# Attention with ternary weights and a gated feed-forward on one core: two-bank places for the ramp's maxima, a new order of the first key chunks, and block work put at other steps

## The chip, the core and the metric

The kernel runs on one core of one Trainium2 chip. The metric is the device time of one execution in microseconds, median of three runs. The core has five engines that work side by side, each through its own queue in order: TensorE (PE; its weight loads are listed as PEld), VectorE (DVE), ScalarE (ACT), GpSimd (POOL) and SyncE (SP), whose queue here issues nearly all DMAs. TensorE writes its results to PSUM, eight banks of 128 partitions x 512 f32.

## The reference

For 4096 tokens of width 256, the kernel computes one attention layer and one feed-forward layer, each with a residual and a layer norm behind it. All inputs are f32.

```python
def quant4(x):                       # per token, 4 bits
    ma = max(max(abs(x), -1), 1e-6)
    return clip(round(x / ma * 7), -8, 7) * ma / 7
def ternary_weight(w):               # -1, 0, 1 times the row's mean magnitude
    thresh = 0.05 * mean(abs(w))
    return where(abs(w) < thresh, 0, sign(w)) * mean(abs(w), axis=1, keepdims=True)

proj = quant4(x) @ ternary_weight(Wqkv).T + b          # one projection for q, k and v
q = proj.reshape(N, 16, 16).transpose(1, 0, 2)         # head h: columns of every token
k = v = proj.reshape(16, N, 16)                        # head h: 256 tokens, cut in 16 parts
q, k = rotary(q), rotary(k)
att = (q @ U) @ (k @ U).T / sqrt(16)                   # 16 heads of 4096 x 4096
y = softmax(att) @ v
x = layernorm(x + quant4(y) @ ternary_weight(Wo).T)
h = silu((x @ w1.T) * s1) * ((x @ w2.T) * s2)          # 256 -> 1024
h = gelu((h @ h1.T) * hs1); h = gelu((h @ h2.T) * hs2)
x = layernorm(x + (h @ w3.T) * s3)
```

## The kernel before

The tokens are cut in eight blocks of 512 (`QB`, `NQB`). The heads go in pairs: a pair's two heads lie in partitions 0 to 63 and 64 to 127 of the keys (`kT`, 128 x 4096) and of a block of queries (`qT`, 128 x 512), so that products of the two use the two halves of the PE array. A unit is one pair and one block of queries; there are 64 units of 32 steps, a step for each 128 keys. Pair 0 comes first with all blocks, so units 0 to 7 are pair 0.

Scores are computed twice. `largest` (L623) takes the maxima: in each step one 128-query tile against 512 keys for both heads, two products into two PSUM banks (L632) and a `tensor_reduce` for each (L640); 32 such steps give the unit's row maxima. These are split in two parts (`largest_parts`, ScalarE and GpSimd, L652 and L653), turned on VectorE (L659), written to DRAM (`m_dram`, L664) and read back as rows (`m_rows`, L667). `weights` (L671) runs `LAG` = 40 steps behind: it subtracts the maxima and adds the scores in PSUM (L678, a two-bank place of pool `ps_sc`, of which there are two) and ScalarE takes the exponential of both heads at once (L686). `values` (L689) comes 4 steps later and adds up the products with v, in four strips (L700). Later `finish`, `turn`, `gather`, `add_strips` and `divide` bring the unit's result in order and to `y_dram`. Hence steps 0 to 39 have only the maxima; this stretch is the ramp.

The order of the work is written by hand: `at(step, f)` puts a function on the list of a step, and the loop at L952 calls a step's list in the order of its making, then `largest` and `weights`. A step's number fixes only each engine's own order; an engine runs ahead until an operand or a buffer holds it.

Queries and keys are not all there at the start. Block b is needed from unit b on, and is prepared in the unit before, from `first = 32 * (b - 1)`: the block's rows of x are loaded (`x_bufs`, two in turn), their maxima taken (`biggest`, `measure`), quantized on GpSimd (`integers`, L148 to L152), transposed (`transposed`, L158, L160), and projected (`even_odd`, L459, ScalarE L467, GpSimd L468 and L469). L468 needs the token scales, which `tables` sends through DRAM (`start_scales`: turned on VectorE, L442, written, L445, read back, L447) together with the block's table of angles (`load_tables`). GpSimd rotates them (`queries`, L484 to L492; `rotate_keys`, L510 to L513); `store_queries` (L497) writes the queries to `q_dram`, and `load_queries` (L583) reads them as the `qT` of a unit, four DMAs. `regroup_keys` moves the rotated keys, `times_g` multiplies them with U's Gram matrix (L529, ScalarE L531, VectorE L532), and `store_keys` (L570) writes them for the other pairs, eight DMAs of a block. `natural` (L170, L603) and `rest` (L606, L607, GpSimd) make the block's v. The matrices of block 0 are prepared ahead of step 0, by VectorE and ScalarE; `place_queries` and `place_keys` put its queries and keys in place by products with selecting matrices, 512 keys at a time (L558, L565), g = 0 to 7.

Three pools of PSUM are used: `ps_sc` (two places of two banks), `ps_av` (one bank) and `ps_1` (three banks), from which `largest` and all block work (`bank1`) take their banks. Pools with one buffer (`kprep`, `rot`, `quantp`) make a block's first writer wait for the last reader of the block before.

The weights of the output layer are made ternary ahead of step 0: `magnitudes` (ScalarE L101, four products with ones, L104) and `signs` (VectorE, L113 to L120). They are first used in `front_steps`, at the attention's end. After the units comes the feed-forward (L964 on).

Of the kernel before, what the change touches and what calls it, by code (L numbers as in the profile page):

```python
# [18 lines left out]
P = 128  # L19
# [18 lines left out]
def attn_ffn_kernel(  # L38
# [54 lines left out]
    alpha_o = const.tile([P, D], F32, name="alpha_o")  # L93
    bias_bc = const.tile([P, D], F32, name="bias_bc")
# [204 lines left out]
    with ExitStack() as actx:  # L299
# [40 lines left out]
        def set_up():  # L340

            nc.sync.dma_start(out=x_bufs[0], in_=x_t[:, ts(0, BT), :])
            tw = [ppool.tile([P, 2, D], F32, name=f"tw{i}", tag="pr") for i in range(2)]
            wabs = ppool.tile([P, 2, 2, D], F32, name="tabs", tag="pr")
            neg = ppool.tile([P, 2, 2, D], F32, name="tneg", tag="pr")
            nc.sync.dma_start(out=tw[0], in_=wqkvT.rearrange("(k p) o -> p k o", p=P))
# [14 lines left out]
            ps = magnitudes(tw[0], wabs[:, 0], bank1)  # L361
# [5 lines left out]
            nc.sync.dma_start(out=tw[1], in_=woT.rearrange("(k p) o -> p k o", p=P))  # L367
# [3 lines left out]
            for e in range(2):  # L371
                for k in range(2):
                    nc.tensor.matmul(
                        ps[:, D + e : D + e + 1],
                        lhsT=wabs[:, 0, k, e::2],
# [15 lines left out]
            signs(tw[0], neg[:, 0], ps, sgn_qkv, alpha_qkv)  # L391
            nc.vector.tensor_scalar(alpha2, ps[:, D : D + 2], 1.0 / D, None, ALU.mult)
            nc.vector.tensor_tensor(gmat, psg[:, :P], mask, ALU.mult)

            def output_weights():
                ps = magnitudes(tw[1], wabs[:, 1], bank1)
                return lambda: signs(tw[1], neg[:, 1], ps, sgn_o, alpha_o)

            return held, output_weights
# [148 lines left out]
        def place_keys(held, kT, g, banks={}):  # L548

            if g % 2 == 0:  # L550
                banks[0] = ps_sc.tile([P, 2, QB], F32, name="sc")
            ps = banks[0][:, g % 2]
# [70 lines left out]
        def largest(s):  # L623

            u, i = divmod(s, NKT)
            qt, ck = divmod(i, NKT // BT)
            if i == 0:
                mxs[u] = stat.tile([P, BT, 2, NKT // BT], F32, name="mx")
            ps = [ps_1.tile([P, 512], F32, name="ps1") for j in range(2)]
# [9 lines left out]
            for j in range(2):  # L639
                nc.vector.tensor_reduce(  # L640
                    mxs[u][:, qt, j, ck : ck + 1], ps[j], AX.X, ALU.max
                )
# [174 lines left out]
        with tc.manual_schedule():  # L817
# [6 lines left out]
            first_held, output_weights = set_up()  # L824
            even_odd(0, first_held, 0)
            even_odd(0, first_held, 1)
            output_signs = output_weights()
# [5 lines left out]
            times_g(0, first_held, 0)  # L833
            place_queries(first_held, qTs[0])
            place_keys(first_held, kTs[0], 0)
            output_signs()
            times_g(0, first_held, 1)
            for g in range(1, 8):
                at(g - 1, lambda g=g: place_keys(first_held, kTs[0], g))
# [4 lines left out]
            for b in range(1, NQB):  # L844
# [13 lines left out]
                else:  # L858
                    biggest(None)
                    for f in measure:  # L860
                        f()
# [311 lines left out]
```

## Time and profile before

| | |
|---|---|
| three runs | 3588.69 to 3589.31 us, median 3589.16 |
| the profiled execution | 3586.87 us, its span 3585.0 |
| mean granted clock of TensorE | 0.993 |
| PE busy | 3544.8 us (99%) |
| DVE busy | 3044.8 us (85%), of it L640 2550.0 |
| ACT busy | 2337.1 us (65%), of it L686 1991.6 |
| POOL busy | 432.2 us (12%) |
| DMA moved | 141.74 MB |
| first issues of `m_dram` (one for a unit, its step 35) | 82.08, 133.53, 184.34, 236.37, 289.39, 339.99, 390.29, 434.55, 478.07 us |

Times are counted from the span's start. A row of the timeline has the start, the time, the engine, the line, the operation, output and inputs, the shapes and, in brackets, how long the engine stood idle ahead of it and what ended this. Rows that follow each other closely are merged (x4); their time is then that of the whole row. A row of the waits has the sum, how often, and the longest. In the forty slices a digit is a tenth, and 9 stands for 90% or more. A busy PE is not PE at its peak, since matmuls are pipelined and their ends are modelled.

### The profile page before, as it was taken

Reading aid. Unit: us, or ns where it says so; the run is one execution under the profiler, and the core shown is the slowest. Engines: PE = TensorE matmul, PEld = TensorE weight load, DVE = VectorE, ACT = ScalarE, POOL = GpSimd, SP = SyncE. Lnnn points to the kernel's source line nnn. Section 1 sums busy time; section 2 is a strip of 40 time slices with the busy share of each in tenths; the row PEclk is TensorE's granted clock in tenths of the full one; section 3 lists DMA queues with packets and bytes.
Section 4 is the critical chain, followed back from the end, with each engine's and each line's share of the span. In section 5 each row is a group of like instructions: output and inputs, shape, how many; then the busy total and the mean of one; then the engine's idle time right before and its main releaser. Section 6 shows DMA issues by size and latency. Waiting matters only on the chain.

```text
span 3585.0 us, 61100 instructions
## 1 busy us (share of the span) xinstructions
PE 3544.8 (99%) x23824; PEld 1996.1 (56%) x23831; DVE 3044.8 (85%) x5612; ACT 2337.1 (65%) x2710; POOL 432.2 (12%) x525
## 2 busy tenths in 40 slices
PE   7999999999999999999999999999999999999998
PEld 4444455555555555555555555545555458888887
DVE  8888999999999999999999999999999945555554
ACT  2777777777777777777777777777777753333332
POOL 5766300000000000000000000000000010000000
PEclk7999999999999999999999999999999999999999
DMA  3343212111211121112111111211121130000000
GB/s 92 91 112 100 58 27 50 27 27 27 50 27 29 30 50 27 27 27 51 28 27 43 34 27 27 44 27 23 47 68 33 24 91 1 29 25 18 18 7 13
DMA packets 267634, 141.74 MB, mean 40 GB/s; under 512 B 184520, under 2 KB 243656, under 8 KB 266440
## 3 DMA queue, kind: packets, MB, share of 16 engines
q1 hardware_dynamic: 263512, 126.22, 14.3%
q0 software_dynamic: 3824, 11.54, 1.1%
q8 instruction: 189, 3.10, 0.4%
q14 instruction: 109, 0.89, 0.1%
HBM read 91.44 MB, written 42.07 MB: 37 GB/s over the span
## 4 chain that ended last, share of the span: by engine, by line
PE 93%; POOL 2%; DVE 2%; DMA 2%; ACT 0%; issue 0%; SPq 0%; POOLq 0%; ACTq 0%
PE av L700 27%; PE sc L678 25%; PE ps L632 21%; PE ps_mm L997 18%; DVE mx L640 1%; DMA qT<-q_dram 1%; DMA scale<-ma_dram 0%; PE ps L529 0%; DMA ma_dram<-ma_turned 0%; POOL eo L469 0%; POOL qk L492 0%; POOL eo L468 0%; DMA q_dram<-qk 0%; POOL rot L484 0%; POOL rot L485 0%
## 5 line engine op out<-in xcount | busy, mean ns | idle before, releaser
L640 DVE TENSOR_REDUCE mx<-ps 128x1 f32<-128x512 f32 x4096 | 2550.0, 683 | 147.4 <-PE ps L632 93.1
L686 ACT ACTIVATE pr<-sc 128x1024 f32<-128x1024 f32 x2048 | 1991.6, 1021 | 739.4 <-PE sc L678 737.2
L632 PEld LDWEIGHTS ps<-kT,qT 64*128 64x128 f32 x4096 | 567.3, 184 | 985.2 <-DVE mx L640 852.1
L700 PE MATMUL av<-pr,v_all 128*32 128x512 f32 x8192 | 1091.6, 605 | 0.7
L632 PE MATMUL ps<-kT,qT 64*128 64x512 f32 x4096 | 1064.5, 474 | 10.0 <-DMA qT<-q_dram 4.0
L678 PE MATMUL sc<-m_rows,minus 64*128 64x512 f32 x4096 | 821.6, 394 | 0.4 <-DMA m_rows<-m_dram 0.4
L678 PE MATMUL sc<-qT,kT 64*128 64x512 f32 x4096 | 816.3, 392 | 0.0
L678 PEld LDWEIGHTS sc<-m_rows,minus 64*128 64x128 f32 x4096 | 392.6, 185 | 88.0 <-ACT pr L686 36.1
L678 PEld LDWEIGHTS sc<-qT,kT 64*128 64x128 f32 x4096 | 392.9, 184 | 86.7
L700 PEld LDWEIGHTS av<-pr,v_all 128*32 128x32 f32 x8192 | 161.3, 108 | 256.6 <-issue 254.7
L1027 ACT ACTIVATE gate<-ps_mm,sc_hs 128x512 f32<-128x512 f32 x128 | 88.1, 689 | 288.7 <-PE ps_mm L997 248.6
L281 DVE CAST h<-gate 128x512 fp32r<-128x512 f32 x128 | 54.3, 425 | 223.6 <-ACT gate L1027 223.4
L653 POOL TENSOR_TENSOR m_parts<-m,m_parts 128x8 fp32r<-128x8 f32 x64 | 13.0, 203 | 1798.7 <-ACT m_parts L652 1763.5
L283 DVE TENSOR_TENSOR h<-gate,h 128x512 fp32r<-128x512 f32 x192 | 132.3, 689 | 5.1
L997 PE MATMUL ps_mm<-h,h1a 128*128 128x512 f32 x512 | 128.8, 394 | 0.0
L1019 DVE SCALAR_TENSOR_TENSOR gate<-ps_mm,sc_s,gate 128x512 f32<-128x512 f32 x64 | 48.0, 750 | 94.3 <-ACT gate L1017 74.3
L997 PE MATMUL ps_mm<-h,h2a 128*128 128x512 f32 x512 | 127.2, 390 | 0.0
L997 PE MATMUL ps_mm<-h,h1b 128*128 128x512 f32 x512 | 126.5, 389 | 0.0
L997 PE MATMUL ps_mm<-h,h2b 128*128 128x512 f32 x512 | 126.5, 389 | 0.0
L732 DVE STREAM_TRANSPOSE yt<-ya 128x64 f32<-128x64 f32 x504 | 116.8, 232 | 0.0
L997 PEld LDWEIGHTS ps_mm<-h,h1b 128*128 128x128 f32 x512 | 96.1, 188 | 20.1
L997 PEld LDWEIGHTS ps_mm<-h,h2b 128*128 128x128 f32 x512 | 96.1, 188 | 19.9
(178 smaller groups left out, 1636.8 us busy)
## 6 DMA issues: line engine op xcount, KB each, us to landing
y_raw<-yt SPq DMA_DIRECT2D x256, 64.0 KB
qT<-q_dram SPq DMA_DIRECT2D x252, 64.0 KB
y<-y_raw SPq DMA_DIRECT2D x63, 256.0 KB
kT<-k_dram SPq DMA_DIRECT2D x28, 512.0 KB
xs<-in_x SPq DMA_DIRECT2D x16, 512.0 KB
q_dram<-qk SPq DMA_DIRECT2D x32, 256.0 KB
k_dram<-qk SPq DMA_DIRECT2D x56, 128.0 KB
cs_q<-in_csq SPq DMA_DIRECT2D x8, 512.0 KB
```

Source lines behind the costliest of these rows:

```text
L281: eng(dst[:, k, 0, :], g)
L283: nc.vector.tensor_tensor(dst[:, k, 1, :], g, dst[:, k, 0, :].bitcast(F32), ALU.subtract)
L632: nc.tensor.matmul(ps[j], lhsT=qTs[u][rows, ts(qt, P)], rhs=kTs[u // NQB][rows, ts(ck, 512)], start=True, stop=True,)
L640: nc.vector.tensor_reduce(mxs[u][:, qt, j, ck : ck + 1], ps[j], AX.X, ALU.max)
L653: nc.gpsimd.tensor_tensor(parts[:, :, 1, :], m, parts[:, :, 0, :].bitcast(F32), ALU.subtract)
L678: nc.tensor.matmul(ps[:, j, :], lhsT=minus[rows, :] if first else kTs[u // NQB][rows, ts(kt, P)], rhs=m_rows[u % 2][rows, :] if first else ...
L686: nc.scalar.activation(pr, ps, AF.Exp)
L700: nc.tensor.matmul(avs[u][strip : strip + 32, :], lhsT=v_all[:, 2 * (2 * pair + j) + a, c * (DK + 1) : c * (DK + 1) + 32], rhs=probs[s + k ...
L732: nc.vector.transpose(yts[u][:, ts(i, 64)], yas[u][:, ts(i, 64)])
L997: nc.tensor.matmul(ps, lhsT=sb[:, ks, ts(o, P)] if split else wo[:, k, :], rhs=src[:, k, i, :], start=(k == 0 and i == 0), stop=(k == n - ...
L1019: nc.vector.scalar_tensor_tensor(g, pb, scales["s2"][:, o : o + 1], gate, ALU.mult, ALU.mult)
L1027: nc.scalar.activation(g, ps, AF.Gelu, scale=scales[sc][:, o : o + 1])
```

## The change

- In the ramp (steps below 40) `largest` takes a two-bank place of `ps_sc` instead of two banks of `ps_1`, and one `tensor_reduce` takes the maxima of both heads from it. Later steps are as before.
- In unit 0 the maxima go by key chunk (four query tiles of a chunk, then the next chunk) instead of by query tile. `place_keys` uses `bank1`, and chunk g is placed at step 2g - 2 instead of g - 1.
- The output weights are loaded at step 3, into a tile of the pool `quantp`; their sums are taken at step 20 (ScalarE, TensorE, ScalarE), and their signs at step 288 on GpSimd.
- The second block's rows are measured and quantized ahead of `place_queries`; the first block's second `times_g` goes to step 5, its `rest` to step 34, its `natural` to steps 0 and 2, its `store_queries` to step 3.
- A block's steps come from a table `t`, with rows for block 1, block 2 and the others: tables, transposed, two even_odd, queries, store_queries, rest, natural, rotate_keys, regroup_keys. `integers` of block 2 goes from -1 to +2. `load_queries` of units 3 to 7 goes from 25 to 22.

```diff
@@ set_up, and a new output_weights
-            tw = [ppool.tile([P, 2, D], F32, name=f"tw{i}", tag="pr") for i in range(2)]
...
-            nc.sync.dma_start(out=tw[1], in_=woT.rearrange("(k p) o -> p k o", p=P))
...
-            def output_weights():
-                ps = magnitudes(tw[1], wabs[:, 1], bank1)
-                return lambda: signs(tw[1], neg[:, 1], ps, sgn_o, alpha_o)
...
+            def load():
+                held["w"] = quantp.tile([P, 2, 2, D], F32, name="two", tag="yb")
+                nc.sync.dma_start(
+                    out=held["w"][:, 0], in_=woT.rearrange("(k p) o -> p k o", p=P)
+                )
+            def sums():
+                ps = magnitudes(held["w"][:, 0], held["w"][:, 1], bank1)
+                nc.scalar.activation(
+                    alpha_o, ps[:, :D], AF.Copy, scale=1.0 / D, accum_out=total_o
+                )
+            def steps():
+                w, a = held["w"][:, 0], held["w"][:, 1]
+                th = stat.tile([P, 1], F32, name="tth")
+                nc.gpsimd.tensor_scalar(th, total_o, 1.0 / D, 0.05, ALU.mult, ALU.mult)
+                nth = stat.tile([P, 1], F32, name="tnth")
+                nc.gpsimd.tensor_scalar(nth, th, -1.0, None, ALU.mult)
+                nc.gpsimd.tensor_scalar(a, w, nth, None, ALU.is_le)
+                nc.gpsimd.tensor_scalar(w, w, th, None, ALU.is_ge)
+                nc.gpsimd.tensor_tensor(sgn_o, w, a, ALU.subtract)
@@ place_keys
-            if g % 2 == 0:
-                banks[0] = ps_sc.tile([P, 2, QB], F32, name="sc")
-            ps = banks[0][:, g % 2]
+            ps = bank1([P, QB], F32)
@@ largest
-            qt, ck = divmod(i, NKT // BT)
+            qt, ck = divmod(i, NKT // BT) if u else divmod(i, BT)[::-1]
...
-            ps = [ps_1.tile([P, 512], F32, name="ps1") for j in range(2)]
+            both = ps_sc.tile([P, 2, QB], F32, name="sc") if s < LAG else None
+            ps = [
+                ps_1.tile([P, 512], F32, name="ps1") if both is None else both[:, j]
+                for j in range(2)
+            ]
...
+            if both is not None:
+                nc.vector.tensor_reduce(mxs[u][:, qt, :, ck], both, AX.X, ALU.max)
+            else:
+                for j in range(2):
+                    nc.vector.tensor_reduce(
+                        mxs[u][:, qt, j, ck : ck + 1], ps[j], AX.X, ALU.max
+                    )
@@ the order
-            output_signs = output_weights()
...
+            h, biggest, measure, integers, transposed = quantize_steps(
+                x_bufs[1], bank1, nc.gpsimd, ma_parts[1][:, :BT]
+            )
+            biggest(None)
+            for f in measure:
+                f()
+            integers()
+            second = h, transposed
             place_queries(first_held, qTs[0])
             place_keys(first_held, kTs[0], 0)
-            output_signs()
-            times_g(0, first_held, 1)
             for g in range(1, 8):
-                at(g - 1, lambda g=g: place_keys(first_held, kTs[0], g))
-            at(2, lambda: store_queries(0, first_held))
+                at(2 * g - 2, lambda g=g: place_keys(first_held, kTs[0], g))
             for i in range(2):
-                at(4 + i, lambda i=i: natural(0, first_held, 2 * i))
-            at(6, lambda: [f() for f in first_held["rest"]])
+                at(2 * i, lambda i=i: natural(0, first_held, 2 * i))
+            at(3, lambda: store_queries(0, first_held))
+            at(5, lambda: times_g(0, first_held, 1))
+            at(34, lambda: [f() for f in first_held["rest"]])
+            load, sums, steps = output_weights()
+            at(3, load)
+            at(20, sums)
+            at(NKT * (NQB + 1), steps)
...
-                at(first - 1 if b > 1 else 0, integers)
-                at(first + 5, tables)
-                at(first + 7, transposed)
+                    at(first + 2 if b == 2 else first - 1, integers)
...
+                t = {
+                    1: (0, 3, 5, 6, 7, 21, 36, 13, 16, 29),
+                    2: (9, 11, 13, 15, 16, 24, 21, 17, 20, 30),
+                }.get(b, (-2, 5, 7, 9, 10, 21, 15, 11, 14, 28))
+                at(first + t[0], tables)
+                at(first + t[1], transposed)
                 for o in range(2):
-                    at(first + 9 + 2 * o, lambda b=b, h=h, o=o: even_odd(b, h, o))
-                at(first + 12, lambda b=b, h=h: queries(b, h))
-                at(first + 23, lambda b=b, h=h: store_queries(b, h))
+                    at(first + t[2 + o], lambda b=b, h=h, o=o: even_odd(b, h, o))
+                at(first + t[4], lambda b=b, h=h: queries(b, h))
+                at(first + t[5], lambda b=b, h=h: store_queries(b, h))
                 for i in range(2):
-                    at(first + 13 + 2 * i, lambda b=b, h=h, i=i: natural(b, h, 2 * i))
-                at(first + 16, lambda b=b, h=h: rotate_keys(b, h, nc.gpsimd))
-                at(first + 17, lambda h=h: [f() for f in h["rest"]])
-                at(first + 29, lambda h=h: regroup_keys(h))
+                    at(first + t[7] + 2 * i, lambda b=b, h=h, i=i: natural(b, h, 2 * i))
+                at(first + t[8], lambda b=b, h=h: rotate_keys(b, h, nc.gpsimd))
+                at(first + t[6], lambda h=h: [f() for f in h["rest"]])
+                at(first + t[9], lambda h=h: regroup_keys(h))
...
-                    at(NKT * (u - 1) + (25 if u < NQB else 14), lambda u=u: load_queries(u))
+                    at(NKT * (u - 1) + (25 if u < 3 else 22 if u < NQB else 14), lambda u=u: load_queries(u))
```

## The prediction

> **What bounds the kernel now.** I read the forty slices of the page first, then windows cut at the places where the work changes, then the timelines of the engines over the first 140 us, and the waits from 90 to 440 us. A step is one pass of the loop at L952; 32 steps are a unit; step 0 begins at 29.15 us.
>
> ```profile
> PE   7999999999999999999999999999999999999998
> DVE  8888999999999999999999999999999945555554
> POOL 5766300000000000000000000000000010000000
> PEclk7999999999999999999999999999999999999999
> ```
>
> TensorE is full from slice 2 on and VectorE nearly so until the attention ends. Only the first five slices (448 us) have GpSimd work, and only there does the diff move anything.
>
> ```profile
> 29.15:41.30 12.15, 11.01 (x72) 8.04 (x72) 9.56 (x17) 5.41 (x12) 8.21 (x9) 1.00 0.02 3
> 41.30:75.90 34.60, 32.04 (x74) 14.80 (x73) 33.50 (x60) 4.48 (x9) 31.68 (x29) 0.64 0.32 91
> 75.90:89.30 13.40, 11.98 (x27) 4.59 (x26) 9.98 (x19) 1.37 (x3) 4.67 (x5) 0.50 0.14 44
> 184.30:236.40 52.10, 50.20 (x345) 24.20 (x344) 44.04 (x86) 36.65 (x45) 35.40 (x32) 1.00 0.55 134
> 434.60:478.10 43.50, 43.50 (x322) 21.60 (x322) 41.47 (x75) 32.80 (x38) 4.47 (x5) 1.00 0.14 33
> ```
>
> Columns: window, length, busy PE, PEld, DVE, ACT, POOL, granted clock, DMA share, GB/s. The first three rows are the ramp (steps 0 to 39), where only maxima are taken: from 41.30 to 75.90 VectorE works 33.50 of 34.60 us, so it sets the pace there, and TensorE is granted half its clock from about 51 us. The fourth row is a unit that also prepares a block of queries and keys (52.10); the fifth is a plain one (43.50, TensorE never idle).
>
> ```profile
> 20.75 1.22 DVE L485 TENSOR_TENSOR rot<-eo,cs_q 128x1024 f32<-128x1024 f32 x1
> 53.84 2.48 DVE L640 TENSOR_REDUCE mx<-ps 128x1 f32<-128x512 f32 x4 [0.63 <-PE ps L632]
> 22.19 2.04 PE L529 MATMUL ps<-keys,gmat 128*128 128x512 f32 x2 [3.56 <-DMA keys<-rk]
> 27.17 1.02 PE L529 MATMUL ps<-keys,gmat 128*128 128x512 f32 x2
> 82.11 2.07 PE L529 MATMUL ps<-keys,gmat 128*128 128x512 f32 x2
> ```
>
> Four maxima in a row take 2.48 us: 0.69 for the last and 0.597 from one to the next. The same product takes 1.02 us at full clock and 2.07 in the ramp's last third; by its 2.04 at 22.19 the start runs at half clock too.
>
> ```profile
> 148.28 1.27 POOL L468 TENSOR_TENSOR eo<-eo,scale 128x512 f32<-128x512 f32 x1 [15.03 <-DMA scale<-ma_dram]
> 182.73 1.04 POOL L152 TENSOR_SCALAR qint<-qtmp 128x1024 bf16<-128x1024 f32 x1
> 183.85 0.21 POOL L653 TENSOR_TENSOR m_parts<-m,m_parts 128x8 fp32r<-128x8 f32 x1
> ```
>
> ```profile
> 136.23 5.12 SPq L570 DMA_DIRECT2D k_dram<-qk  x8
> 141.46 0.53 SPq L445 DMA_DIRECT2D ma_dram<-ma_turned  x1
> 144.97 0.36 SPq L447 DMA_DIRECT2D scale<-ma_dram  x1
> ```
>
> ```profile
> PE ps L632 <- DMA qT<-q_dram: 4.0, 3, 1.7
> DVE m_turned L659 <- POOL m_parts L653: 2.9, 4, 1.2
> ```
>
> In a block, GpSimd waits 15.03 us for the scales, whose request stood behind eight key stores in SP's queue (5.12 us), then works 35.6 us without a pause, and the unit's maxima (`m_parts`) come last in its queue. Their two late products, queries (`qT`) and maxima, stop TensorE and VectorE (last two lines).
>
> **The change, part by part.** Start. VectorE loses the output weights' signs (five operations, 25.50 to 27.94) and does the second block's maxima there instead (1.21, 0.16, 0.18 us from 25.6). TensorE loses one L104 group (2.08) that lay beside VectorE work. With `times_g` gone from 27.17 and the two `place_keys` in banks of their own, step 0's products are done near 29.6, and its maxima start then instead of at 30.98: 1.3 us won.
>
> Steps 0 to 15. From 27.3 TensorE's queue holds seven `place_keys` (1.17 each: 8.2), sixteen pairs of L632 (0.47: 7.5), four `natural` (0.6: 2.4), the transposes (0.7), `times_g` (1.0), two `even_odd` (0.6: 1.2): 21.0 us, plus some 1.7 for the wait for GpSimd's `qint` at step 3 and for places: to 50.0, and the maxima end near 51.4. VectorE alone would need 29.6 + 16 x 1.14 + 0.7 = 48.6, so TensorE sets the pace here. Before, step 15 ended at 55.13: 3.7 won. The second block's `queries`, now at step 7, reuse the buffer that `place_keys` read until step 12; GpSimd comes to its first write there at 37.7 + 5.7 + 7.3 = 50.7 (from `even_odd` at step 5, by the rows from 148.28 on), after the last of them at 46, so it doesn't wait.
>
> The merged maximum, 128x2 from 128x1024, is not in the trace. From above: two of the old (1.195 from step to step). From below: L485's 128x1024, whose start is 1.14 after the like operation at 19.61. I take 1.14, the row of the same size; nothing excludes 1.20, since at half clock a place's round (1.22 for the maximum, 0.8 to 1.0 to refill it) comes to 1.0 to 1.1 for each of two places.
>
> [...]
>
> Steps 16 to 31: 16 x 1.14 = 18.2, plus 1.6 for the next block's maxima (four of 0.41 and two small), plus the output weights' sums: four L104 at half clock, 2.08 us in TensorE's queue. A pair of L632 there takes 0.8 (0.79 at 84.12); filling, sums and refilling take 0.85 + 2.08 + 0.85 against two maxima's 2.28: 1.5 us of stall. ScalarE's two operations (0.61, and 0.4 to 0.7 by L603 and L467 with 0.19 for the accumulator) have an idle engine. So step 31 ends near 72.7 instead of 75.69.
>
> The granted clock is 0.50 from 52 to 88 us with TensorE shown busy 3.3 to 4.0 us in every 4, so I take half clock. [...]
>
> Steps 32 to 39: 8 x 1.14, twice a `times_g` for which VectorE waits (2.07 + 0.59 ScalarE + 0.69 own, less what is filled ahead: 2.0 each), 0.5 of small ones: 13.7, to 86.5 instead of 91.28: 4.8 ahead.
>
> What takes over: block 2's chain on GpSimd. Its tables now stand at step 41, behind the key stores (81.8 to 86.9): `ma_turned` near 87.7, scales 7.5 later as before (89.99 to 97.45): 95.2. `even_odd` at step 45 comes at 94.6, 95.7 with ScalarE. GpSimd is free then: the first block's `rest` (5.5), `integers` (5.3) and the second's `rest` (5.5) follow `m_parts` at about 75 and end at 91.5. Then 35.6 us as before: `m_parts` at 131.3 instead of 133.05, while VectorE would come to `m_turned` at 86.5 + 40.8 (91.28 to 132.09 before) + 0.7 (the transposes, now behind step 40) = 128.0. So of 4.8 us 1.75 remain, and VectorE waits some 3 us for `m_parts`, with the maxima of the next steps queued behind, and TensorE behind those.
>
> Blocks 3 to 7. Scales are asked for at step -2, before the key stores, and GpSimd starts with step 7's `even_odd`, 14 us into the unit (12.7 us for seven steps of unit 2, 1.4 for product and ScalarE) instead of 21.7 (148.28 less 126.6). Queries then arrive 14 + 29 = 43 us into a unit of 50 (29 from GpSimd's start, 200.34, to `qT`, 229.3), and its chain, with `rest` (5.5) now before the end, leaves `m_parts` free. Both waits go. From `m_dram` issue to issue (133.53, 184.34, 236.37, 289.39, 339.99, 390.29, 434.55) the units last 50.81, 52.03, 53.02, 50.60, 50.30, 44.26. Without its 0.8 of `qT` wait the fifth is 49.5; the four before it have four L129 maxima more, which widen a step by 0.15 each: 50.1. Won: 0.7 + 1.9 + 2.9 + 0.5 + 0.8 = 6.8. The last holds only `times_g` and stays. TensorE's extra work is the same, only sooner; SP's wait for the write of `ma_dram` (3.5 us) ends before step 3 needs `m_dram`.
>
> The output signs on GpSimd: three of about 1.57 (L469) and two tiny ones, in a unit where it is busy 4.5 of 43.5 us and nobody waits; if they fell before an `m_parts`, 5 us once. The load of the weights is one issue of 0.5 on SP with nothing due behind it. Nothing else moves.
>
> Sum: 1.75 + 6.8 = 8.6. The profiled execution took 3586.87 (span 3585.0), so 3578.3; the median of the three runs is 3589.16, 2.3 above it, so 3580.6. A difference of 0.2% (7.2 us) is about what a measurement of this kernel can tell from none.
>
> **The rivals.** More: block 2's chain isn't last, because the sums don't stall and GpSimd starts three to five microseconds sooner; then the ramp's 4.8 to 6.3 pass through: 3574 to 3577. For it: three of my terms there are rounded up. Against: the scales' path of 7.5 us is all queue and transfer. 0.16.
>
> Less: the waits in blocks 3 to 7 are replaced rather than removed (scales early, but ScalarE, full of exponentials, hands over `even_odd` late, or SP stands at `load_queries`, now three steps sooner, with the regrouped keys behind it). Half of 6.8 is lost, and the ramp's 1.75 may go too: 3584 to 3588. For it: units two and six had few such waits and are still over 49.5. 0.17.
>
> Slower: TensorE doesn't get its full clock at 27 us. It rose just after the products of 22.19 to 27.33, and the change takes one product out behind them. At half clock the 21.0 us of steps 0 to 15 become 35 (`natural` 1.01 against 0.61) to 42 (L529), 14 to 21 us more, all ahead of block 2's chain: 3595 to 3601. It decides against the change if half clock lasts past about 40 us. Against it: `place_keys` follow without a pause. 0.09.
>
> **How the numbers follow.** The forecast (3577.5 to 3583) has 0.58, three quarters of it below 3582, which is 0.2% under the median. With the first rival that makes faster 0.60; the rest of the forecast and "less" make same 0.31; slower has 0.09. The range leaves out the slow case and the edge of the best: 3574 to 3588.
>
> **What would show it.** Right: 40 maxima 128x2 from 128x1024, 1.14 apart; L104's second group in the ramp at 2.08; `m_dram`'s second issue at 131 to 132.5 with VectorE waiting some 3 us for `m_parts` before it; no wait for `qT` or `m_parts` in later units, which last 49.5 to 50.3; scales issued before the key stores. Wrong: clock below 1.00 between 30 and 45 us; maxima 1.2 apart or more; second `m_dram` before 130 or after 133.5; units still over 51; any GpSimd work delaying `m_parts` after 440 us.

## The result, and the profile after

The changed kernel takes 3577.81 us (median of nine runs, 3576.94 to 3579.56). The kernel before, run beside it, takes 3587.68 (nine runs, 3586.15 to 3589.31). The ratio is 0.9973, 95% interval 0.9964 to 0.9981: 9.9 us or 0.27% less, and the interval does not reach 1. The profiled executions, 3577.81 (span 3575.9) and 3586.87 (span 3585.0), differ by 9.1, and all of that is there when the attention's last maxima end: 2850.25 against 2859.35 us. The prediction said 3580.6.

In the page's forty slices GpSimd's row differs from before in the first five alone, where it is now 5, 7, 7, 6 and 2. The fifth falls from 3 to 2: the last block's work ends at 369.8 us instead of 385.6.

The windows of the changed kernel, cut at like places of the work (about steps 0 to 5, 6 to 31, 32 to 39, then the unit that prepares block 4; columns as before). The third row goes to the ramp's end; the third row of before ended at 89.30, with step 38, two microseconds short of it.

```profile
28.90:40.00 11.10, 9.34 (x57) 5.63 (x56) 8.01 (x8) 5.83 (x11) 5.72 (x6) 1.00 0.73 239
40.00:71.90 31.90, 22.48 (x88) 10.77 (x88) 30.84 (x33) 4.69 (x12) 21.53 (x15) 0.70 0.21 58
71.90:83.60 11.70, 9.10 (x24) 3.65 (x25) 10.61 (x12) 1.37 (x3) 10.50 (x14) 0.65 0.12 34
179.80:230.20 50.40, 49.69 (x347) 24.07 (x344) 43.81 (x85) 36.62 (x44) 35.33 (x31) 1.00 0.53 130
```

The ramp's forty steps last 54.7 us (28.90 to 83.6) instead of 60.3 (30.98 to 91.28). The unit that took 52.10 takes 50.40; VectorE, ScalarE and GpSimd are as busy in it as before (43.81, 36.62, 35.33), so no work has left them. TensorE's idle time in it falls from 1.90 to 0.71 us, and its shown busy time by the other 0.5. Units without a block's work take what they took.

VectorE's and TensorE's timelines in the ramp:

```profile
39.76 12.54 DVE L667 TENSOR_REDUCE mx<-sc 128x2 f32<-128x1024 f32 x11 [0.94 <-PE sc L659]
54.53 2.07 PE L105 MATMUL ps<-two,ones 128*128 128x256 f32 x4
72.61 2.07 PE L552 MATMUL ps<-keys,gmat 128*128 128x512 f32 x2
75.76 1.60 PE L552 MATMUL ps<-keys,gmat 128*128 128x512 f32 x2
130.14 0.21 DVE L689 STREAM_TRANSPOSE m_turned<-m_parts 128x32 f32<-128x32 f32 x1 [2.35 <-POOL m_parts L683]
```

Eleven merged maxima take 12.54 us: 1.22 for the last and 1.13 from one to the next, without a gap. The sums of the output weights (L105) run at half clock (0.50 from 52.9 to 76.8 us). The two `times_g` take 2.07 and 1.60 where the second took 2.07 before, since the clock came back at 76.8. Ahead of 130.14 VectorE has stood for 2.35 us, waiting for block 2's `m_parts`.

What stands ahead of that, on GpSimd and in SP's queue:

```profile
94.37 1.28 POOL L491 TENSOR_TENSOR eo<-eo,scale 128x512 f32<-128x512 f32 x1 [5.14 <-DMA scale<-ma_dram]
129.90 0.20 POOL L683 TENSOR_TENSOR m_parts<-m,m_parts 128x8 fp32r<-128x8 f32 x1
```

```profile
85.22 0.51 SPq L892 DMA_DIRECT2D xs<-in_x  x1
85.83 0.53 SPq L468 DMA_DIRECT2D ma_dram<-ma_turned  x1
90.95 0.35 SPq L470 DMA_DIRECT2D scale<-ma_dram  x1
120.86 0.60 SPq L468 DMA_DIRECT2D ma_dram<-ma_turned  x1
133.02 5.05 SPq L591 DMA_DIRECT2D k_dram<-qk  x8
```

Block 2's chain (94.37 to 129.90) is 35.5 us of uninterrupted GpSimd work that waited for its scales to start. Block 3's scales are asked for at 120.86, ahead of the eight key stores at 133.02 and not behind them. The waits of the changed kernel from 88 to 440 us that replace those shown of before are these two, both at block 2; none follows after 133 us:

```profile
DVE m_turned L689 <- POOL m_parts L683: 2.3, 1, 2.3
PE ps L659 <- DMA qT<-q_dram: 0.7, 1, 0.7
```

The account by `m_dram` marks (a mark is the issue on SP after a unit's maxima). First mark 82.08 before, 77.35 after: 4.7 won. Second 133.53, 130.38: 3.15 left of that. The six units from there last 49.41, 50.40, 50.41, 50.38, 49.81, 44.23 (294.6) instead of 301.0: 6.4 won. From then on both kernels take the same time, but for 0.4 us in 2850.

The same by steps (a step ends when its last maximum does) shows where the ramp's lead went. At the end of step 39 the changed kernel is 7.7 us ahead (83.55 against 91.28), of step 63 it is 5.3 (121.30 against 126.58), of step 95 it is 3.2 (174.18 against 177.36). The second loss, 2.1, falls where block 2's late products are waited for. The first, 2.4, falls before any such wait. The rows are steps 40 to 63 in the kernel before, in the changed kernel, and in run 11 below, which has the changed kernel's code there and a full clock:

```profile
91.28:126.58 35.30, 33.77 (x240) 17.29 (x244) 31.34 (x55) 25.67 (x31) 28.29 (x23) 0.99 0.35 96
83.55:121.30 37.75, 37.13 (x247) 19.46 (x243) 31.63 (x56) 26.83 (x32) 31.52 (x28) 0.91 0.33 98
81.34:116.88 35.54, 34.14 (x241) 17.20 (x241) 31.45 (x57) 26.43 (x32) 29.95 (x25) 1.00 0.31 91
```

In the changed kernel the clock comes back at 90.4 us, almost when it did before (91.6), and so 7 us behind the ramp's end and not with it. These steps also hold block 2's transposes, for which VectorE waited in step 39 before (2.07 us for that step, 1.19 for the one ahead of it). With them and a full clock the steps take 35.54, so some 2.2 us of the lead went to half clock.

### The profile page after: what moved, and what is told of

Read it like the earlier page. It is cut to its first block, busy times and chain, and to the rows that moved or that the text cites. A ratio compares the mean times of both kernels' runs of the same rounds, so it can differ in the third digit from the quotient of the medians.

```text
span 3575.9 us, 61056 instructions
## 1 busy us (share of the span) xinstructions
PE 3527.8 (99%) x23831; PEld 1987.6 (56%) x23831; DVE 3042.4 (85%) x5566; ACT 2337.7 (65%) x2712; POOL 437.0 (12%) x530
## 4 chain that ended last, share of the span: by engine, by line
PE 96%; DVE 2%; DMA 1%; POOL 1%; ACT 0%; issue 0%; SPq 0%; POOLq 0%; ACTq 0%; DVEq 0%
PE av L730 28%; PE sc L708 26%; PE ps L659 22%; PE ps_mm L1042 18%; DVE mx L667 1%; DVE mx L670 1%; PE ps L552 0%; PE ps L482 0%; PE ps L171 0%; PE ps_mm L1084 0%; PE ps_mm L171 0%; PE ps_mm L289 0%; DVE qk L555 0%; DMA qT<-q_dram 0%; ACT pr L716 0%
## 5 line engine op out<-in xcount | busy, mean ns | idle before, releaser
L670 DVE TENSOR_REDUCE mx<-ps 128x1 f32<-128x512 f32 x4016 | 2501.5, 684 | 138.1 <-PE ps L659 86.2
L659 PEld LDWEIGHTS ps<-kT,qT 64*128 64x128 f32 x4016 | 549.5, 183 | 952.3 <-DVE mx L670 831.2
L659 PE MATMUL ps<-kT,qT 64*128 64x512 f32 x4016 | 1023.4, 470 | 2.2 <-DVE mx L670 1.4
L284 DVE TENSOR_TENSOR h<-gate,h 128x512 fp32r<-128x512 f32 x192 | 132.5, 690 | 5.1
L1042 PE MATMUL ps_mm<-h,h1b 128*128 128x512 f32 x512 | 126.6, 389 | 0.0
L1042 PEld LDWEIGHTS ps_mm<-h,h1b 128*128 128x128 f32 x512 | 96.1, 188 | 20.4
L1042 PEld LDWEIGHTS ps_mm<-h,h2b 128*128 128x128 f32 x512 | 96.1, 188 | 20.0
## 6 DMA issues: line engine op xcount, KB each, us to landing
k_dram<-qk SPq DMA_DIRECT2D x56, 128.0 KB
```

Source lines behind the costliest of these rows:

```text
L284: nc.vector.tensor_tensor(dst[:, k, 1, :], g, dst[:, k, 0, :].bitcast(F32), ALU.subtract)
L659: nc.tensor.matmul(ps[j], lhsT=qTs[u][rows, ts(qt, P)], rhs=kTs[u // NQB][rows, ts(ck, 512)], start=True, stop=True,)
L670: nc.vector.tensor_reduce(mxs[u][:, qt, j, ck : ck + 1], ps[j], AX.X, ALU.max)
L1042: nc.tensor.matmul(ps, lhsT=sb[:, ks, ts(o, P)] if split else wo[:, k, :], rhs=src[:, k, i, :], start=(k == 0 and i == 0), stop=(k == n - ...
```

## The experiments

All edits are to the changed kernel unless said otherwise; none leaves work out. In the table of steps `t`, the places stand for tables, transposes, first and second `even_odd`, `queries`, `store_queries`, `rest`, `natural`, `rotate_keys` and `regroup_keys`. Where no number of runs is given, the time is that of one execution. Where an effect is near 1 us it is read from marks inside the trace: from the ninth mark to the end, where the code is the same in all of them, the profiled executions took from 3106.9 to 3109.3 us.

**1. The steps of blocks 3 to 7 as before.**

```diff
-                }.get(b, (-2, 5, 7, 9, 10, 21, 15, 11, 14, 28))
+                }.get(b, (5, 7, 9, 11, 12, 23, 17, 13, 16, 29))
-  at(NKT * (u - 1) + (25 if u < 3 else 22 if u < NQB else 14), ...load_queries(u))
+  at(NKT * (u - 1) + (25 if u < NQB else 14), ...load_queries(u))
```

> The changed kernel with blocks 3 to 7 (and load_queries of units 3 to 7) put back to the steps they had before; ramp and blocks 1 and 2 stay changed. Theory (the later blocks' own steps removed the waits for qT and m_parts): the first two m_dram issues stay at 77.4 and 130.4 us, the six intervals after them grow from 294.6 us in sum to 299 to 301, and the span from 3575.9 to 3580 to 3582.5. Rival (the lead from the ramp had cured those waits): the six intervals stay within 1 us of 294.6 and the span within 1 us of 3576.

3585.24 us (11 runs), ratio 0.9992 (0.9983 to 1.0001); span 3583.0. The six units take 52.21, 52.05, 51.65, 51.82, 48.88, 44.27: 300.9. Its waits from 133 to 440 us:

```profile
DVE m_turned L689 <- POOL m_parts L683: 7.2, 4, 2.3
PE ps L659 <- DMA qT<-q_dram: 0.6, 1, 0.6
```

The wait for the maxima comes back in four units. Without the new steps the kernel loses 6.2 us after the ramp by the marks (7.4 by the medians), nearly all that the change won there. The forecast held for the units. The span was half a microsecond above it, and the second mark (131.08) 0.7 late, after a half-clock window from 124.6 to 128.1 that the changed kernel's trace does not have.

**2. Only these steps, in the kernel before.** The reverse edit in the kernel before, for blocks above 2 and queries of units 3 to 7.

> The kernel before with nothing but the new steps of blocks 3 to 7 and of load_queries in units 3 to 7. Theory: the first two m_dram issues stay at 82.1 and 133.5 us, the six intervals shrink from 301.0 to about 294.6, the span from 3585.0 to 3578 to 3579.5; what is left to the changed kernel's 3575.9 is the ramp's. Rival (these steps help only when block 2 comes early): the intervals stay over 299 and the span over 3583.

3584.06 us (11 runs), ratio 0.9987 (0.9978 to 0.9996); span 3580.8. The units take 50.40, 50.37, 50.40, 50.37, 49.82, 44.22: 295.6, and no wait for queries or maxima is left after 133 us. That is the changed kernel's 294.6 but for 1.0 in the first of them, which in the changed kernel is short because the mark that it is counted from, 130.38, is itself late (run 4). So 5.4 are won here and not 6.4. The span missed by 1.3 us, for that and because the ramp, whose code is that of before, was 0.8 us longer in this execution: TensorE dropped to half clock at 46.5 us instead of 50.7 and stayed there to 97.7 instead of 91.6.

**3. Two maxima of 512 again, but in the two-bank place.**

```diff
-                nc.vector.tensor_reduce(mxs[u][:, qt, :, ck], both, AX.X, ALU.max)
+                for j in range(2):
+                    nc.vector.tensor_reduce(
+                        mxs[u][:, qt, j, ck : ck + 1], both[:, j], AX.X, ALU.max
+                    )
```

> The changed kernel, but in the ramp two maxima of 512 from a two-bank place instead of one of 1024. Theory (in the VectorE-bound steps an instruction saved is 0.06 to 0.07 us of each step, and block 2's chain starts from the ramp's end, so it passes on): step time 1.20 instead of 1.13 in steps 7 to 33, the ramp's last maximum ends at 85.5 to 86.2 instead of 83.55, second m_dram at 132.3 to 133 instead of 130.4, span 3577.8 to 3578.6. Rival 1 (at half clock the refilling of two places sets the step): last maximum within 0.5 us of 83.55. Rival 2 (the ramp's lead is swallowed by block 2's chain): last maximum later, second m_dram within 0.5 us of 130.4.

3580.18 us, span 3578.4. Its VectorE timeline:

```profile
39.85 13.25 DVE L668 TENSOR_REDUCE mx<-sc 128x1 f32<-128x512 f32 x22 [0.88 <-PE sc L659]
```

Twenty-two in 13.25 us: 1.20 a step against 1.13. Step 39 ends at 85.60 (83.55 with the merged ones) and the second `m_dram` is at 132.81 (130.38). Merging is worth 2.05 us at the ramp's end. How much of it passes on is not cleanly shown: step 63 ends 1.3 us later than in the changed kernel (122.59), and the 2.4 at the mark hold a half-clock window from 124.3 to 127.7, behind a `qT` wait of 1.8.

**4. Block 2's `rest` later**, so that its maxima don't queue behind it.

```diff
-                    2: (9, 11, 13, 15, 16, 24, 21, 17, 20, 30),
+                    2: (9, 11, 13, 15, 16, 24, 34, 17, 20, 30),
```

> The changed kernel with block 2's rest (eight GpSimd operations, 5.6 us) put at step 66 instead of 53, that is behind the m_parts of unit 1. Theory (GpSimd's chain of block 2 holds m_parts, and VectorE and TensorE wait for it): VectorE's wait of 2.4 us before m_turned goes, second m_dram at 127.5 to 128.3 instead of 130.4, span 3573.2 to 3574. Rival (something else in step 67 is last, such as times_g, or the wait moves to step 71): second m_dram moves by less than 1 us, or the interval after it grows by what was won, and the span stays within 0.7 us of 3575.9.

3579.14 us, span 3577.4. The maxima are ready at 124.59 and VectorE's wait for them is gone, but from 118 to 134 us the waits and VectorE's timeline hold

```profile
PE ps L659 <- DMA qT<-q_dram: 1.9, 1, 1.9
129.17 0.20 DVE L689 STREAM_TRANSPOSE m_turned<-m_parts 128x32 f32<-128x32 f32 x1
```

and step 95 ends at 174.18, as in the changed kernel (174.18). The second mark comes at 129.40, 1.0 sooner (forecast 2 to 3), and the unit behind it is 1.0 longer (50.41), as the rival had it. My theory that the 2.35 us wait was the limit fell: queries and maxima are two late products of one chain, and taking one away leaves the other.

**5. Block 2's tables earlier**, the first 9 of that row as -2.

> The changed kernel with block 2's tables (its scales) at step 30 instead of 41, as the later blocks have them. Theory (block 2's late products, qT and m_parts, both hang on the start of its GpSimd chain, and that start on the scales at 94.37): the chain starts with ScalarE's even_odd near 93.1, second m_dram 1.0 to 1.3 us earlier (129.1 to 129.4 instead of 130.38), the wait for qT at step 64 shorter as well, span 3574.5 to 3575. Rival (the scales are no longer last: GpSimd's rest or ScalarE are): second m_dram within 0.4 us of 130.38.

3579.32 us, span 3577.5 (forecast 3574.5 to 3575). GpSimd starts at 93.49 instead of 94.37, and the second `m_dram` moves by 0.26 us though the ramp was 0.34 longer. The scales are asked for at 71.8, but now GpSimd waits for ScalarE's `even_odd` (92.72 and 96.29), which comes with the products of steps 45 and 47. The mark moved as little as the rival said. A new wait had taken the place of the old one: the chain's start needs tables, transposes and a free GpSimd together.

**6. The bulk load behind the scales.** Block 3's 512 KB of x are issued just ahead of the 16 KB write of `ma_dram` (85.22 and 85.83 above).

```diff
-                        first - 24,
+                        first - (20 if b == 3 else 24),
```

> The changed kernel with the load of block 3's rows (512 KB) at step 44 instead of 40, so behind block 2's tables in SP's queue instead of just ahead. Theory (this load shares the DMA engines with the small write of the scales, which took 5.1 us from issue to the next issue where it took 3.3 before): 3.0 to 3.5 us again, block 2's chain starts near 93.1 instead of 94.37, second m_dram at 129.1 to 129.4. Rival (the eight key stores ahead of it cause it): 4.5 us or more again, second m_dram within 0.4 us of 130.38.

3579.01 us, span 3577.2. SP's queue:

```profile
85.62 0.53 SPq L468 DMA_DIRECT2D ma_dram<-ma_turned  x1
88.46 0.36 SPq L470 DMA_DIRECT2D scale<-ma_dram  x1
89.54 0.59 SPq L892 DMA_DIRECT2D xs<-in_x  x1
```

The write's time to the next issue is 2.84 us instead of 5.12: the load ahead stretched it. GpSimd starts 1.2 sooner (93.18) and is then held by ScalarE's `even_odd`, as in run 5; the second `m_dram` comes only 0.5 sooner (forecast 1.0 to 1.3), and step 95 ends 1.1 later (175.27), with a half-clock window at 132.1 to 135.5. The write takes 5.5 in run 11 with the load ahead again, and 3.3 in the kernel before, where the load comes behind. So the load ahead is the cause of the stretch; taking it away isn't worth anything alone.

**7. The output weights' sums at the start**: `load()` after `set_up`, `sums()` after the first `even_odd`, instead of steps 3 and 20.

> The changed kernel with the output weights' load and sums ahead of step 0, where the kernel before had them; their signs stay on GpSimd at step 288. Theory (the sums cost one stall of 1.13 us in step 20 and nothing at the start): step 20 back from 2.26 to 1.13, the ramp's last maximum at 82.3 to 82.6 instead of 83.55, second m_dram at 129.1 to 129.5, span near 3574.8. Rival (at the start they delay the first key products): the first maximum later than 28.9 by 0.5 us or more and little left of the gain.

3578.48 us, span 3576.7. Step 20 lasts 1.13 instead of 2.26, the first maximum still starts at 28.90, step 39 ends at 82.57 (0.98 sooner), the second `m_dram` is at 129.17 and step 95 ends at 173.04 (1.14 sooner). The sums cost 1.1 us where they stand, all of it passed on to step 95, and nothing at the start. The span does not show it (forecast 3574.8): from the ninth mark to the end this execution took 1.9 us more than the changed kernel's.

**8. TensorE's early work later**: the second block's transposes and `even_odd` from step 9, the first block's `natural` from step 7.

```diff
-                at(2 * i, lambda i=i: natural(0, first_held, 2 * i))
+                at(7 + i, lambda i=i: natural(0, first_held, 2 * i))
-                    1: (0, 3, 5, 6, 7, 21, 36, 13, 16, 29),
+                    1: (0, 9, 10, 11, 12, 21, 36, 13, 16, 29),
```

> The changed kernel with the first block's natural at steps 7 and 8 instead of 0 and 2, and block 1's transposes, even_odd and queries at 9, 10, 11 and 12 instead of 3, 5, 6 and 7. Theory (TensorE sets the pace up to step 6, with VectorE idle 4.1 us there): steps 3 to 6 shrink from 8.6 us to 5 to 6.5, steps 7 to 15 grow by at most 1, the ramp's last maximum ends at 81 to 82.5 instead of 83.55. Rival (the products only move the stall to where they go, or block 1's queries come too late for step 32): steps 3 to 15 within 0.7 us of 18.8 in sum, or a wait for qT at step 32.

3578.41 us, span 3576.6. Steps 3 to 6 fall from 8.59 to 6.25 us, steps 7 to 15 rise from 10.18 to 11.93: 0.6 won of 18.8, which is no more than executions differ in whose code is the same up to there (17.85 to 18.77 in the changed kernel and runs 9, 11 and 12). The work moved with its price, which is the rival's forecast. Step 39 ends at 83.21, but the second `m_dram` is 0.4 later than in the changed kernel (130.82), after a `qT` wait of 1.9 and a half-clock window at 123.2 to 126.6.

**9. The whole of block 2's chain sooner.** Tables, transposes and `even_odd` earlier, and `rest` of both blocks off GpSimd's path.

```diff
-                    1: (0, 3, 5, 6, 7, 21, 36, 13, 16, 29),
-                    2: (9, 11, 13, 15, 16, 24, 21, 17, 20, 30),
+                    1: (0, 3, 5, 6, 7, 21, 98, 13, 16, 29),
+                    2: (-2, 8, 9, 11, 12, 22, 34, 13, 16, 30),
```

> The changed kernel with block 2's GpSimd chain made earlier and shorter: its tables at step 30, its transposes, even_odd and queries at 40, 41, 43 and 44 (from 43, 45, 47, 48), its rest behind m_parts at step 66, and block 1's rest at step 98 (from 36). Theory (both late products of that chain, qT and m_parts, cost the first steps of unit 2 12.0 us instead of the 9.5 of unit 3; taking away one alone left the other): the chain starts at 87 to 89 instead of 94.37, no wait for qT or m_parts near step 64, steps 64 to 68 take 9.5 to 9.8 us, step 95 ends at 171.5 to 172.2 instead of 174.18, time 2 to 2.7 us under the changed kernel. Rival (these steps are bound by TensorE's own products, times_g above all): 11.4 us or more again, step 95 within 0.7 us of 174.2.

3576.50 us (7 runs), ratio 0.9970 (0.9958 to 0.9981); span 3576.7. GpSimd starts at 88.09, both waits are gone, and steps 64 to 68 take 9.49 us instead of 12.01, the same as in unit 3. But step 63 ends at 124.26, 3.0 later than in the changed kernel, and step 95 at 174.60, 0.4 later: in the profiled execution, the slowest of the seven, the 2.5 us are lost before they are won. The median is 1.3 under the changed kernel's (forecast 2 to 2.7), but the two intervals lie nearly on each other, so this gain isn't shown. The window of this kernel shows where the time went:

```profile
84.00:96.00 12.00, 11.47 (x43) 6.03 (x42) 6.04 (x10) 6.94 (x8) 5.90 (x5) 0.50 0.33 99
```

TensorE now has the block's work at the ramp's end while its clock is still at half (until 96.1; 90.4 in the changed kernel): step 40 takes 3.94 us (1.89 there), steps 41 to 45 take 2.0 to 2.57 (1.29 to 2.08).

**10. Runs 9 and 7 together.**

> The same, and the output weights' load and sums ahead of step 0. Theory: the two gains add, since the ramp's end shifts all that follows: step 95 ends at 170.3 to 171.2, time 3.0 to 3.8 us under the changed kernel. Rival: once block 2's chain is early, the ramp's 1.1 us no longer shows: within 0.4 us of the run without it.

3575.39 us (6 runs), ratio 0.9967 (0.9954 to 0.9979); span 3573.1. Step 95 ends at 170.91, inside the forecast and 3.3 ahead of the changed kernel; the median is 2.4 under it, short of the 3.0 to 3.8 forecast. The same window, with the clock back at 86.5:

```profile
84.00:96.00 12.00, 10.47 (x61) 5.22 (x58) 8.46 (x14) 8.87 (x12) 8.15 (x6) 0.90 0.26 81
```

It holds 61 counted pieces of TensorE's work where run 9 holds 43, with TensorE less busy. That the sums' place moved the clock's return isn't shown; it moves between executions of the same code too (91.6 us in the kernel before, 97.7 in run 2).

**11. TensorE kept busy in the ramp.** One product more in each of the steps 16 to 39, read by nobody.

```diff
+            def warm():
+                nc.tensor.matmul(
+                    bank1([P, 512], F32)[:, :D], lhsT=ones, rhs=alpha_qkv, start=True, stop=True
+                )
+            for s in range(16, LAG):
+                at(s, warm)
```

> The changed kernel with one product more in each of the steps 16 to 39, ones by 128x256 f32, whose result nobody reads (about 0.52 us at full clock, 1.04 at half). Theory (TensorE is granted half its clock in the ramp because its products, though shown busy, fill too little of the time, and the sums and times_g stall VectorE only for that): granted clock 1.00 from about 55 to 90 us, step 20 below 1.5 us, steps 34 and 36 together 1.2 to 2 us shorter than 4.6, steps else 1.13, the ramp's last maximum at 81 to 82.5. Rival (half clock whatever fills the time, as no idle gap explains it): steps of 1.8 to 1.9 us from 16 on, the last maximum at 95 us or later.

3577.97 us, span 3576.2. The windows of the changed kernel and of this one, over the half-clock stretch:

```profile
52.00:90.00 38.00, 28.41 (x84) 13.14 (x86) 33.76 (x42) 6.03 (x10) 25.70 (x28) 0.56 0.32 91
```

```profile
52.00:90.00 38.00, 35.48 (x155) 16.90 (x154) 36.84 (x47) 8.73 (x14) 25.79 (x28) 1.00 0.33 91
119.60:126.40 6.80, 5.12 (x16) 1.81 (x17) 1.98 (x3) 0.81 (x1) 6.46 (x8) 0.50 0.40 107
```

The clock is full from 27.4 to 119.6 us. The four sums take 1.13 instead of 2.07 and no longer stall a maximum (step 20: 1.16), both `times_g` steps fall to 1.73, step 39 ends 2.2 us sooner (81.34) and step 63 4.4 sooner (116.88). Then the work arrives at a chain that moved by only 1.65: GpSimd starts at 92.72, its write of scales stretched to 5.5 us again. TensorE waits 2.7 us for `qT`, loses the clock for 6.8 (last line), and steps 64 to 68 take 16.7 us instead of 12.0. Step 95 ends at 174.48 (174.18): all 4.4 are given back.

**12. Chain sooner and TensorE busy**: run 9's `rest` at 98, block 2 at `(-2, 9, 10, 12, 13, 22, 34, 14, 17, 30)`, and run 11's products.

> The changed kernel with block 2's chain freed (tables at step 30, transposes, even_odd and queries at 41, 42, 44 and 45, its rest at 66, block 1's rest at 98) and one unread product of ones by 128x256 f32 in each of the steps 16 to 39; the sums stay at step 20. Theory (full clock wins 4.4 us by step 63, which block 2's chain gave back at step 64, and freeing the chain alone won 2.5): the two add once both are there: step 63 ends at 116.8 to 118, steps 64 to 68 take 9.5 to 10.5 us, step 95 ends at 167 to 168.5 (174.18 in the changed kernel), time 5 to 7 us under the changed kernel. Rival (the chain still ends no earlier than 120 us): a wait for qT at step 64, step 95 at 170 or later.

3571.65 us (5 runs, 3571.41 to 3572.82), ratio 0.9956 (0.9943 to 0.9970); span 3570.8. Step 39 ends at 81.44, step 63 at 118.66 (0.7 above the forecast, with a half-clock window at 82.8 to 86.2), steps 64 to 68 take 9.48, and step 95 ends at 169.03, 5.2 ahead of the changed kernel (0.5 above the forecast). Around the former wait, 13 us from just ahead of the end of step 63, in the changed kernel and here:

```profile
121.00:134.00 13.00, 11.05 (x64) 4.42 (x65) 8.16 (x15) 7.79 (x10) 8.54 (x10) 1.00 0.29 84
```

```profile
118.40:131.40 13.00, 12.39 (x84) 5.39 (x82) 10.32 (x19) 9.56 (x12) 6.99 (x11) 1.00 0.33 104
```

TensorE is idle for 0.6 us there instead of 2.0, and 84 of its pieces are done instead of 64. Run 9's and run 11's edits alone leave step 95 where it was (174.60 and 174.48 against 174.18); together they bring it 5.2 us forward, and 6.2 in the median: each removes the limit that hid the other. This version beats both kernels, 16 us under the kernel before; its runs and the changed kernel's do not overlap.

## Why the prediction was right, point by point

**Start and steps 0 to 15.** Right, a little too careful. The first maxima start at 28.90 (predicted 29.6) and step 15 ends near 51.1 (51.4). A part of the first figure is chance: with the same work up to there they start between 28.90 and 29.86 (the changed kernel and runs 1, 3 to 6, 9, 11 and 12). Step 15 still ends between 51.16 and 51.26 in all of them but run 3, which takes two maxima a step. Its shape was wrong: TensorE does not set the pace throughout. Steps 3 to 6 stall (2.60, 1.55, 2.27, 2.17 us), and from step 7 VectorE runs 1.13 without a gap. Run 8 found that the stalled work costs nearly the same at later steps. GpSimd's first write into the shared buffer comes at 50.88 (predicted 50.7), without a wait. The rival of a start at half clock did not come: the clock is 1.00 from 25.6 to 52.9 us. No run takes back the order of the key chunks or the second block's earlier start alone, so how the 4.0 us won by step 15 (55.13 to 51.17) divide among the parts of the change stays open.

**The merged maximum.** Predicted 1.14, measured 1.13. Run 3 prices it at 2.05 us over the ramp; forty steps of the prediction's 1.14 instead of the 1.195 that two maxima took before make 2.2. In the kernel before, maxima in a row overlap by 0.09 us (0.69 for the last, 0.597 from one to the next), which a count of single rows does not hold.

**The sums.** Predicted 1.5 us of stall at half clock, measured 1.13, and 0.98 to 1.14 by run 7. Step 31 ends at 71.83 (72.7).

**Steps 32 to 39.** Predicted 2.0 for each `times_g`, measured 1.73 for one (step 34: 2.86) and 0.6 for the other (step 36: 1.73): the clock returned between them. The end, 83.55, is 2.9 better than the 86.5 of the prediction; 7.7 us ahead of before and not 4.8. Not all of this is gain: the transposes that stood at step 39 now come behind it.

**The clock.** The prediction took half clock for the ramp from the rows of before (0.50 with TensorE shown busy), and it came: half clock from 52.9 to 76.8 and from 80.2 to 90.4. In the changed kernel no gap of TensorE's is over 0.64 us from 40 us to that fall at 52.9. Run 11 shows that the clock hangs here on what fills the steps: one short product more in each (0.6 to 0.7 us) kept 1.00. Which property of it counts isn't separated: the share of time, or that it is 128 x 128 where the products of the maxima are 64 x 128. The busy time of the profile alone does not tell: the kernel before is shown busy for all of 68 to 76 us and stays at 0.50.

**Block 2's chain.** The mechanism was right. Chain start 94.37 (95.7), length 35.5 (35.6), maxima at 129.90 (131.3), VectorE's wait 2.35 (3). What was mis-sized is the share that remains: 3.15 us, not 1.75: the chain ended 1.4 sooner than predicted, nearly all of it from its start. The ramp's end was 2.9 sooner, of which 1.3 us reached the chain's start; from the write of `ma_dram` to the chain's start it took 8.5 us and not 7.5, since the write was stretched (run 6). That VectorE came to the maxima almost when predicted (127.79 against 128.0) is luck: it started from a ramp that ended 2.9 sooner, and needed 44.2 us and not 41.5. The term of 40.8 + 0.7 was taken from a kernel whose clock was full from 91.6 us on, 0.3 behind its ramp, and had nothing for half clock behind a ramp that ends sooner. The prediction named the wait for `m_parts` as what would come next. Run 4 shows that as half of the truth: the `qT` of the same chain is 1.9 late once the maxima are not.

**Blocks 3 to 7.** Predicted 6.8, measured 6.4 (units of 50.4 instead of 50.1); 1.0 of this is only the lateness of the mark at 130.38, from which they are counted, and run 2 wins 5.4. The rival "replaced rather than removed" did not come: no `qT` or `m_parts` wait is left after 133 us, and run 1 brings them back. A part of the gain was not waiting itself: in the kernel before, the unit of 53.02 also holds a stretch at half clock right behind the wait, in its windows

```profile
278.00:282.00 4.00, 2.26 (x16) 1.23 (x12) 2.77 (x6) 2.68 (x4) 3.84 (x6) 1.00 0.78 163
282.00:286.00 4.00, 4.00 (x16) 1.48 (x16) 1.98 (x3) 0.83 (x1) 3.74 (x5) 0.60 0.25 44
```

TensorE stands idle for 1.74 us of the first window; in the second it is busy throughout, at a granted 0.60, and VectorE has only 1.98 us of work.

**The output signs on GpSimd.** Free, as predicted: 1.58, 1.57, 1.28 and two tiny ones from 438.66 to 443.9, with the next maxima 22 us later.

**The sum.** Predicted 8.6, measured 9.1 between the profiled executions: the ramp 1.4 more and the units 0.4 less than in the sum, the rest (0.4) within what single executions differ by. That the two lie so close is in part luck, since the ramp's end was 2.9 off and half clock and the stretched write took some of it back. The time itself is 2.8 under the 3580.6 forecast, most of it from another term: the 2.3 added because the median of three runs stood that far above the profiled execution. The changed kernel's median of nine is its profiled execution's time, and the nine of before have a median only 0.8 above theirs. The first rival (the ramp's whole gain passing through, 3574 to 3577) came partly: the ramp did gain more than the upper end of its 4.8 to 6.3, but half clock behind it and the chain held it back. Of the signs named beforehand, the second mark (130.38) came a little sooner than its 131 to 132.5, the wait was 2.35 and not 3, and the units are 0.1 over their 49.5 to 50.3; none of the signs of being wrong appeared.

## What to carry to other kernels

When two late products hang on one chain, start the chain sooner; moving one of them behind something else only shows the other. A gain in a stage is kept only if the chain that bounds the next stage starts sooner too, so change both before judging either (at step 95 nothing alone, 5.2 us together). Price a wait together with the steps behind it, since a stretch at half clock there can be part of its cost (a granted 0.60 over the 4 us behind the wait of 1.7 in the kernel before). When the same edit can land on a stretch with another clock (0.50 and 0.90 from 84 to 96 us in runs 9 and 10), compare inside the trace, at like steps, and not by the time alone.

## What the runs showed of the hardware

- TensorE can be granted half its clock while the profile shows it busy nearly all the time (11.47 of 12.00 us at 0.50 in run 9), and a product of 0.6 to 0.7 us more in each 1.1 us step kept it at 1.00 (run 11).
- The half-clock stretches measured here last 3.4 us (123.2 to 126.6 in run 8, 132.1 to 135.5 in run 6), 6.8 (119.6 to 126.4, run 11), 10.2 and 23.9 (80.2 to 90.4 and 52.9 to 76.8, changed kernel) and 40.9 (50.7 to 91.6, kernel before). Where they begin differs between executions: ramps of the same code fell to half at 50.7 (kernel before) and 46.5 us (run 2), and these two ramps differ by 0.8 us.
- A wait of 1.7 to 2.7 us for `qT` was followed by a stretch of 3.4 to 6.8 us at half clock in runs 1 (2.0), 3 (1.8), 8 (1.9) and 11 (2.7) and in the kernel before (1.7), but not in run 4 (1.9). In run 6 the stretch came behind a wait of 2.4 us for `m_parts`, and the changed kernel's of 2.35 had none. What decides that stays open.
- A 16 KB write with a 512 KB load issued 0.6 us ahead of it took 5.1 us to the next dependent issue; without the load ahead, 2.84 (run 6).
